# SyncE takes over 15 list fetches and 13 output writes of a graph network kernel, one row a transfer

## The chip, the cores and the metric

The kernel runs on one core of one Trainium2 chip. A core has a matrix engine (PE; its weight loads are listed as PEld), a vector engine (DVE), a scalar engine (ACT), GpSimd (POOL) and SyncE (SP), which computes nothing and issues DMA transfers. Each engine runs its own instructions in order and waits for the others by semaphores. A transfer that an engine issues is carried out by the core's 16 DMA engines.

The metric is the time of one execution on the device, in microseconds (us), as the median over several runs. Before the change it is 3867.69 us over nine runs, from 3839.4 to 3890.41.

## What is computed

A graph with N = 6250 nodes of 256 features and E = 100000 edges, sorted by their target node, goes through three attention layers. For each node they gather rows of the nodes that send it an edge, weigh them by a softmax, and add them up:

```python
# layers 1 and 2 (4 heads of 64, with a loop edge at each node)
xl, xr = x @ Wl, x @ Wr
logits = einsum('ehc,hc->eh', leaky_relu(xl[src] + xr[dst], 0.2), att)
alpha = softmax over the edges of one dst
out[dst] += alpha * xl[src]            # + b; elu after layer 1
# x = layernorm(x + layer 2)
# layer 3 (8 heads of 32)
e = leaky_relu(s1[src] + s2[dst], 0.2)
out[dst] += softmax(e) * Wh[src]
# result = layernorm(x + layer 3)
```

The result has one row of 256 f32 for each node, in the order of the nodes.

## The kernel before

**Plan.** `make_plan` sorts the nodes by their number of edges, most first, and cuts them into 49 blocks of 128, a node a partition. `cols[b]` is the number of edge columns of block b, fixed when the program is built: 27, 25, 24, 23, 22, 21, 21, 20, ... down to 9, 803 in all. What few edges the first block has beyond 27 go another way (`find_few`). `node_i[p, b]` holds the number of the node at partition p of block b. The DRAM table `near_d` has for each node, in the nodes' own order, its list of sources (CM = 38 numbers) followed by its row of x (256 f32): 1176 bytes. A tile `wrong` collects tests of the plan. If any fails, `fits` is 0 and a general path runs in place of `tile_by_degree`.

**Layer 1** (`layer2(0, ...)`). For block b, `start1(b)` has POOL fetch the block's 128 rows of `near_d` by an indirect DMA with `node_i` into `near[:, b, :]` (L1674), three blocks ahead of the work. `gather(b)` issues one indirect DMA on POOL for each column (L1300): 128 rows of a table into one slot of a row tile. Row tiles hold up to 9 columns; the pool has nine of them, so a block takes three (up to block 17) or two. `ready` has PE transpose the block's x rows and make its own terms, `attend` has DVE form the logits (z: L1571, L1591, L1594; lg: L1595) and ACT the exponentials (L1446), `weighted_sum` scales the rows (ACT L1482, DVE L1483) and adds them on PE (L1490), and `finish1` makes the two table rows of layer 2, which SP writes (L1708 and L1709). `finish` of block b - 1 and the last part of `weighted_sum` of block b stand in one round of the loop, the two writes at its end.

**Layer 2** (`layer2(1, ...)`) does the same with lists that are in SBUF by then. It is not touched by the change.

**Layer 3** is the last loop of `tile_by_degree`. A round b issues `gather(b + 1)` on POOL, then `put_out(b - 2)`, also on POOL: an indirect DMA that writes 128 rows of y to the result by `node_i` (L1812). DVE then forms logits (L1782), the products (L1503) and their sums (L1512), and in `between` the layer norm of the block before is made, with ACT writing y (L1534).

Nothing plans the order: `manual_schedule` keeps the instructions on each engine as the code issues them. Waits are put in by the framework. The transfers of SP and ACT go round eight semaphores, and each waits for the last one on its own.

Of the kernel before, what the change touches and what calls it, by code (L numbers as in the profile page):

```python
# [26 lines left out]
F32 = mybir.dt.float32  # L27
BF16 = mybir.dt.bfloat16
I32 = mybir.dt.int32
AF = mybir.ActivationFunctionType  # L30
OP = mybir.AluOpType
AX = mybir.AxisListType
# [3 lines left out]
P = 128  # L36
# [4 lines left out]
RUNS = 64  # L41
EARLY = (14, 12, 11)
LATE = 4


def columns(E, N, NB):

    mean = E / N
    pmf = [math.exp(-mean)]
    for k in range(1, 200):
        pmf.append(pmf[-1] * mean / k)
    over, sd = [], []
    for c in range(199):
        p = sum(pmf[c + 1 :])
        g = sum((k - mean) * pmf[k] for k in range(c + 1, 200))
        over.append(N * p)  # L60
        sd.append(math.sqrt(max(N * (p * (1.0 - p) - g * g / mean), 0.0)))
    cols = []
    for b in range(NB):
        most = P * b
        cols.append(next(
            c for c in range(199) if (over[c] + 3.5 * sd[c] <= most if b else over[c] < 0.01)
        ))
    low = max((c for c in range(199) if N - over[c] <= P // 4), default=0)
    high = next(c for c in range(199) if over[c] <= P // 4)
    pmf += [0.0] * 200  # L70
    held = next(
        c for c in range(199)
        if N * sum((k - c) * pmf[k] for k in range(c, 200))
        + 3.5 * math.sqrt(N * sum((k - c) ** 2 * pmf[k] for k in range(c, 200))) <= P
    )
    assert cols[1] <= held < cols[0]
    return cols, low, high, held


@with_exitstack  # L80
# [634 lines left out]
def make_plan(  # L715
# [6 lines left out]
    nc = tc.nc  # L722
    N, F = x.shape
    E = src.shape[0]
    NB = node_i.shape[1]
    NP = NB * P
    H2, D2 = att[0].shape[1], att[0].shape[2] - 1
    H1, _, D1 = w3.shape
    W2 = H2 * (D2 + 1)
    CM = max(cols)  # L730
    T = 16
    KE = -(-E // (P * T)) * T
# [19 lines left out]
    one = ctx.enter_context(tc.tile_pool(name="plan_one", bufs=1))  # L752
    tmp = ctx.enter_context(tc.tile_pool(name="weights", bufs=2))
    work = ctx.enter_context(tc.tile_pool(name="table1", bufs=3))
    rowp = ctx.enter_context(tc.tile_pool(name="table1_row", bufs=10))
    hot = ctx.enter_context(tc.tile_pool(name="plan_hot", bufs=2))
    ps = ctx.enter_context(tc.tile_pool(name="plan_ps", bufs=1, space=PSUM))
    pst = ctx.enter_context(tc.tile_pool(name="table1_ps", bufs=2, space=PSUM))
# [62 lines left out]
    xs, turned, at = {}, {}, [0]  # L821
# [52 lines left out]
    full, rest = divmod(E, KE)  # L874
# [23 lines left out]
    a = next(d for d in range(512, 0, -16) if E % d == 0)  # L898
# [222 lines left out]
    for k in range(BITS - 2, -1, -1):  # L1121
        n = CM + (1 << k) - 1
# [25 lines left out]
    for k in spans:  # L1148
# [8 lines left out]

    wrong = one.tile([P, KE + 2 * NB + 1], F32, name="wrong")  # L1160
    nc.vector.tensor_tensor(wrong[:, : KE - 1], dst_e[:, : KE - 1], dst_e[:, 1:], op=OP.is_gt)
    nc.vector.tensor_tensor(wrong[:, KE - 1 : KE], dst_e[:, KE - 1 :], next_e, op=OP.is_gt)
    nc.vector.tensor_tensor(wrong[:, KE : KE + NB], got[:, 2, :], most, op=OP.is_gt)
# [5 lines left out]
        wrong[:, KE + NB : KE + 2 * NB], wrong[:, KE + NB : KE + 2 * NB], count  # L1169
    )  # L1170
    nc.vector.tensor_scalar(
        wrong[:, KE + 2 * NB :], base[:, :1], float(E), None, op0=OP.not_equal
    )
    bad = one.tile([P, 2], F32, name="bad")
    nc.vector.reduce_sum(bad[:, :1], wrong, axis=AX.X)
# [32 lines left out]
def tile_by_degree(  # L1208
# [62 lines left out]
    nc.sync.dma_start(wh_d[NP:], nobody[:, 1, :A1])  # L1271


    bias = [fixed[:, 0, :], fixed[:, 1, :]]
    a_src, a_dst = fixed[:, 2, :], fixed[:, 3, :]

# [14 lines left out]

    def source(of, b, j):
        return bass.IndirectOffsetOnAxis(ap=of[:, b, j : j + 1], axis=0)

    def gather_rows(b, rows, cut, own, table, of, width, j0, j1):

# [239 lines left out]
    def layer2(i, table, of, width, start, own, finish, follow):  # L1536
# [5 lines left out]
        with ExitStack() as es:  # L1542
# [9 lines left out]
            def gather(b):  # L1552
# [4 lines left out]
                    gather_few(table, i, width)  # L1557
                state[b] = [rows, cut]

            later = []  # L1560

            def ready(b):
# [72 lines left out]
            for b in range(NB):  # L1635
                if b + 3 < NB:
                    start(b + 3)
                if b + 1 < NB:
                    gather(b + 1)
                if b + 2 == NB:  # L1640
                    follow()
                if b + 1 < NB:
                    ready(b + 1)
                rows, cut, wt, new = attend(b)
                if b:
                    rest = finish(work, pst, b - 1, acc)
                else:
                    new()
                    few = few_sum(work, pst, wt[0], cols[0] + 1, H2, D2 + 1)
                if b:  # L1650
                    new()

                last = []

                def between():
                    if b:
                        last.append(rest())

                acc = weighted_sum(
                    work, ps, rows, cut, wt, H2, D2 + 1, between,  # L1660
                    [bias[0]] if i == 0 else [x1[:, b, :], bias[1]], b == 0,
                )
                if b == 0:
                    nc.tensor.matmul(acc, edges_of, few, start=False, stop=True)
                if last:
                    last[0]()
            finish(work, pst, NB - 1, acc)()()

    def none(t):
# [1 line left out]
        nc.vector.memset(t.rearrange("p (h d) -> p h d", h=H2)[:, :, D2:], -BIG)  # L1671

    def start1(b):
        nc.gpsimd.indirect_dma_start(  # L1674
            out=near[:, b, :], out_offset=None, in_=near_d[:, :], in_offset=node(b)
        )
# [81 lines left out]
    with ExitStack() as es:  # L1758
# [32 lines left out]
        def end(b, acc, den):  # L1791
            h = work.tile([P, F], F32, name="h", bufs=2)
            nc.vector.tensor_mul(
                per_head(h, H1), per_head(acc, H1), den.unsqueeze(2).to_broadcast([P, H1, D1])
            )
            nc.vector.tensor_add(h, h, x1[:, b, :])
            mv, sd = spread_of(work, h)

            def rest():
                y = work.tile([P, F], F32, name="y")  # L1800
                layer_norm(y, h, mv, sd)
                return b, y

            return rest

        gap = work.tile([P, 1], F32, name="gap", bufs=1)
        prod = work.tile([P, 24, F], F32, name="weighted", bufs=1)

        def put_out(b, y, apart):
            if apart:  # L1810
                nc.gpsimd.memset(gap, 0.0)
            put = nc.gpsimd.indirect_dma_start(  # L1812
                out=out[:, :], out_offset=node(b), in_=y, in_offset=None,
                bounds_check=N - 1, oob_is_err=False,
            )
            tc.declare_no_dep(put.ins, group="out", reason="each node has a row of its own")
            tc.add_to_no_dep_group("out", put.ins)

        gather(0)
        acc, den, puts, rest = None, None, {}, None  # L1820
        for b in range(NB):
            if b + 1 < NB:
                gather(b + 1)
            if b - 2 in puts:
                put_out(*puts.pop(b - 2), apart=b + 1 == NB)
            rows, cut, wt, new = attend(b)
            if b:
                rest = end(b - 1, acc, den)
            den = new()
            nc.vector.reciprocal(den, den)  # L1830

            def between():
                if b:
                    puts[b - 1] = rest()

            acc = added_up(work, prod, rows, cut, wt, H1, D1, between)
            if b == 0:
                more = ps.tile([P, F], F32, name="few_acc", tag="tp")
                few = few_sum(work, ps, wt[0], cols[0], H1, D1)
                nc.tensor.matmul(more, edges_of, few, start=True, stop=True)  # L1840
                nc.vector.tensor_add(acc, acc, more)
# [31 lines left out]
```

## Time and profile before

| | us |
|---|---|
| median of 9 runs | 3867.69 |
| lowest, highest | 3839.4, 3890.41 |
| profiled execution | 3886.18 |
| its span | 3884.4 |

Over the span DVE was busy for 2754.9 us (71%), POOL for 2505.1 (64%), PE for 1549.4 (40%) and ACT for 1154.8 (30%). SP has no busy time, since issuing a transfer is not counted. The DMA engines moved 395.84 MB, 102 GB/s on average. The plan takes the first 134 us, layer 1 runs to about 1440, layer 2's first full gather stands at 1531 and its last at 2637, and layer 3's gathers run from 2727 to 3838.

How to read the profile: "busy" lines give an engine's share in 40 equal slices of the span, in tenths. A group's line has the code line, engine, operation, what it writes and reads, its count, then the busy time and the mean nanoseconds of one, then the engine's idle time before it and what ended most of that. A line of waits has who waited for whom, the total in us, the number of times and the longest. "issue" is time in which an engine waited for nothing that the profile shows. A line of a timeline has start, duration and the idle time before. A line of one code line's instructions has their count and shortest, median and longest duration in ns. A "q" after an engine's name marks its sequencer, which loads registers, waits and issues transfers.

### The profile page before, as it was taken

To read this page: it belongs to the slowest core of one execution; us is meant where nothing else is said; L and a number is where in the kernel's file an instruction comes from. 1 tells how busy PE (TensorE), PEld (TensorE's weight loads), DVE (VectorE), ACT (ScalarE), POOL (GpSimd) and SP (SyncE) were. 2 spreads that over 40 slices of the span, in tenths; PEclk is the share of its full clock that TensorE was granted. 3 is DMA by queue.
4 is the path that set the end of the run, shared out by engine and by line. 5 is a ranking of instruction groups with operands and counts; after the bars stand their busy time and mean duration, and the time that the engine had idled before them with its cause. 6 is when DMAs were issued, how large, how long until landed. Compare 5 with 4: busy or idle time off the path is not lost.

```text
span 3884.4 us, 24262 instructions
## 1 busy us (share of the span) xinstructions
PE 1549.4 (40%) x5424; PEld 1182.6 (30%) x5424; DVE 2754.9 (71%) x2527; ACT 1154.8 (30%) x4428; POOL 2505.1 (64%) x2588
## 2 busy tenths in 40 slices
PE   7234545536666774566564666665000000000000
PEld 5123444424555553444443444443000000000000
DVE  7546777747888885898886888885686566666665
ACT  3112333424445442343343555653000000000000
POOL 5565556656666645666666666654677777777774
PEclk8566777768888886677777777887555555555555
DMA  9633333333434433334443444433343333333332
GB/s 205 116 89 85 91 87 95 95 87 104 106 103 110 108 84 99 98 105 112 107 110 107 108 116 113 115 104 79 100 108 101 97 97 96 96 97 96 97 96 57
DMA packets 189103, 395.84 MB, mean 102 GB/s; under 512 B 56249, under 2 KB 107963, under 8 KB 188934
## 3 DMA queue, kind: packets, MB, share of 16 engines
q0 software_dynamic: 121392, 339.19, 33.6%
q1 hardware_dynamic: 59858, 53.27, 5.0%
q10 hardware_dynamic: 7700, 1.74, 0.4%
q8 instruction: 47, 0.77, 0.1%
q14 instruction: 106, 0.87, 0.1%
HBM read 354.02 MB, written 40.42 MB: 102 GB/s over the span
## 4 chain that ended last, share of the span: by engine, by line
issue 30%; POOL 23%; DVE 20%; PE 13%; ACT 6%; another core or an unknown queue 4%; DMA 3%; DVEq 0%; POOLq 0%; ACTq 0%; SPq 0%
POOL g L1300 21%; PE acc L1490 11%; DVE z L1594 4%; ACT g L1482 4%; DVE z L1571 4%; DVE lg L1595 3%; DVE z L1591 3%; DVE g L1483 2%; DMA g<-xl_d,near_r 2%; PE pm L1427 2%; POOL out L1812 1%; DVE weighted L1503 1%; POOL piece_of L1016 1%; ACT wt L1446 1%
## 5 line engine op out<-in xcount | busy, mean ns | idle before, releaser
L1300 POOL DMA_INDIRECT g<-xl_d,near_r x1569 | 1484.2, 946 | 881.5 <-issue 459.5
L1490 PE MATMUL acc<-g,ident 128*128 128x256 f32 x3408 | 1040.5, 472 | 800.6 <-issue 324.9
L1490 PEld LDWEIGHTS acc<-g,ident 128*128 128x128 f32 x3408 | 799.7, 241 | 1040.3 <-issue 351.8
L1300 POOL DMA_INDIRECT g<-whs_d,near_r x766 | 795.7, 1039 | 280.9 <-issue 247.7
L1482 ACT ACTIVATE g<-g,by 128x64 f32<-128x64 f32 x2308 | 609.5, 338 | 345.7 <-issue 337.8
L1595 DVE TENSOR_REDUCE lg<-z 128x28 f32<-128x1820 f32 (+4 forms) x234 | 497.3, 2125 | 8.1
L1594 DVE TENSOR_TENSOR z<-z,at 128x1820 f32<-128x1820 f32 (+4 forms) x234 | 496.8, 2123 | 4.7
L1512 DVE TENSOR_REDUCE acc_v<-weighted 128x256 f32<-128x4096 f32 (+15 forms) x49 | 343.7, 7014 | 14.7 <-remote 8.4
L1483 DVE TENSOR_TENSOR g<-g,wt 128x1792 f32<-128x1792 f32 (+8 forms) x234 | 331.7, 1434 | 27.9 <-issue 18.2
L1571 DVE TENSOR_TENSOR z<-g,pr 128x2080 f32<-128x2080 f32 (+4 forms) x96 | 197.9, 2061 | 177.8 <-DMA g<-xl_d,near_r 68.6
L1591 DVE TENSOR_TENSOR z<-g,pr 128x1820 f32<-128x1820 f32 (+3 forms) x138 | 299.6, 2171 | 17.0 <-DMA g<-xl_d,near_r 8.4
L1456 ACT ACTIVATE wt<-lg 128x128 f32<-128x128 f32 (+17 forms) x49 | 14.0, 285 | 854.2 <-DVE top L1439 314.2
L1671 DVE MEMSET pr<- 128x4 f32 x49 | 3.0, 62 | 348.5 <-remote 118.5
L1782 DVE TENSOR_TENSOR lg<-g,s_r 128x56 f32<-128x56 f32 (+4 forms) x111 | 22.2, 214 | 317.2 <-DMA g<-whs_d,near_r 275.3
L1503 DVE TENSOR_TENSOR weighted<-g,wt 128x1792 f32<-128x1792 f32 (+4 forms) x111 | 226.6, 2057 | 0.1
L1422 ACT COPY xT<-pt 128x256 f32<-128x256 f32 x147 | 54.9, 373 | 508.6 <-PE pt L1420 267.1
L1446 ACT ACTIVATE wt<-lg,top 128x19 f32<-128x19 f32 (+14 forms) x392 | 116.0, 296 | 93.9 <-DVE few_at L1607 34.3
L1427 PE MATMUL pm<-wcat,xT 128*128 128x260 f32 x392 | 109.9, 428 | 51.8 <-ACT xT L1422 41.7
L1427 PE MATMUL pm<-wh_cat,xT 128*128 128x272 f32 x196 | 75.8, 521 | 86.7 <-ACT xT L1422 58.7
L1427 PEld LDWEIGHTS pm<-wcat,xT 128*128 128x128 f32 x392 | 77.7, 209 | 75.6 <-ACT xT L1422 50.4
L1427 PE MATMUL pl<-wcat,xT 128*128 128x260 f32 x196 | 62.8, 448 | 78.1 <-issue 45.7
L1812 POOL DMA_INDIRECT out<-y,node_i x49 | 50.5, 1031 | 49.6 <-ACT y L1534 35.6
(250 smaller groups left out, 1665.8 us busy)
## 6 DMA issues: line engine op xcount, KB each, us to landing
g<-xl_d,near_r POOLq DMA_INDIRECT x1569
g<-whs_d,near_r POOLq DMA_INDIRECT x766
whs_d<-row SPq DMA_DIRECT2D x49, 132.0 KB
xl_d<-xl SPq DMA_DIRECT2D x49, 130.0 KB
xl_d<-row SPq DMA_DIRECT2D x49, 130.0 KB
xr_d<-row SPq DMA_DIRECT2D x49, 130.0 KB
two<-xl_d SPq DMA_DIRECT2D x49, 130.0 KB
two<-xr_d SPq DMA_DIRECT2D x49, 130.0 KB
```

The costliest lines, as they stand in the source:

```text
L1300: nc.gpsimd.indirect_dma_start(out=g[:, j + own - s0, :width], out_offset=None, in_=table, in_offset=source(of, b, j),)
L1427: nc.tensor.matmul(pm, xT[:, c, :], w[:, c, :], start=c == 0, stop=c == 1)
L1446: nc.scalar.activation(wt[:, :, h], lg[:, :S, h], AF.Exp, bias=top[:, h : h + 1], accum_out=den[:, h : h + 1],)
L1482: nc.scalar.mul(g4[:, t, h, :], g4[:, t, h, :], by[:, t - m, h : h + 1])
L1483: nc.vector.tensor_mul(g4[:, :m], g4[:, :m], wt[:, s0 : s0 + m, :].unsqueeze(3).to_broadcast([P, m, H, F // H]),)
L1490: nc.tensor.matmul(acc, ident, g4[:, t], start=False, stop=s0 + t == S - 1 and not more)
L1503: nc.vector.tensor_mul(prod[:, s0 - base : s1 - base, :].rearrange("p t (h d) -> p t h d", h=H), g[:, :n, :F].rearrange("p t (h d) -> p t ...
L1512: nc.vector.reduce_sum(part, prod[:, : s1 - base, :].rearrange("p s f -> p f s"), axis=AX.X)
L1571: nc.vector.tensor_max(z, rows[0][:, :n, :W2], xr[:, None, :].to_broadcast([P, n, W2]))
L1591: nc.vector.tensor_max(z, g[:, :n, :W2], xr[:, None, :].to_broadcast([P, n, W2]))
L1594: nc.vector.tensor_mul(z, z, at[:, None, :].to_broadcast([P, n, W2]))
L1595: nc.vector.reduce_sum(lg[:, s0:s1, :], z.rearrange("p t (h d) -> p t h d", h=H2), axis=AX.X)
```

## The change

Two functions choose blocks when the program is built. `rows_in` takes blocks of layer 1 from block 6 on as fast as 2.6 rows for each column of earlier blocks allow: 6, 8, 11, 13, 16, 18, 21, 24, 27, 30, 33, 36, 40, 43, 47. `rows_out` takes blocks of layer 3 with at least 128 / 2.6 = 49 columns between them: 0, 3, 6, 9, 12, 15, 18, 21, 25, 29, 33, 37, 41.

For these blocks POOL's indirect DMA goes, and SP moves each of the 128 rows by a transfer of its own: 1920 in layer 1 and 1664 in layer 3. The row's place in DRAM comes from a register. `row_starts` makes a tile of the places once in each of the two layers: `node_i` times the row's bytes on DVE, a transpose on PE, a copy on DVE, so that a block's 128 numbers stand in one partition. `numbers_of` has SP load 32 of them into registers at a time. The DRAM tensors are seen as bytes, so the number is the offset.

In layer 1 the rows are issued in the order of the blocks, `int(cols[b] * 2.6)` at the end of each round of the loop, behind that round's two table writes in SP's queue. In layer 3 a taken block's 128 rows are issued where its y is made, each with a `nop` before it. The y of taken blocks has a tile of its own, and the other blocks' y tiles go from three to two. One more test in `wrong` makes sure that no block but the last holds a number without a node.

```diff
+U8 = mybir.dt.uint8
+ALONG = 2.6
+def rows_in(cols):
+    taken, room = [], 0.0
+    for b in range(5, len(cols)):
+        room += cols[b - 5] * ALONG
+        if room >= P:
+            taken.append(b)
+            room -= P
+    return taken
+def rows_out(cols):
+    taken, free, past = [], 0.0, 0
+    for b, n in enumerate(cols):
+        past += n
+        if past >= free and sum(cols) - past >= P / ALONG + 2 * n:
+            taken.append(b)
+            free = past + P / ALONG
+    return taken
...
-    wrong = one.tile([P, KE + 2 * NB + 1], F32, name="wrong")
+    wrong = one.tile([P, KE + 3 * NB], F32, name="wrong")
...
+    nc.vector.tensor_scalar(
+        wrong[:, KE + 2 * NB + 1 :], node_i[:, : NB - 1], float(N), None, op0=OP.is_ge
     )
...
+    def row_starts(work, ps, turned, width, bufs):
+        scaled = work.tile([P, F], F32, name="h", bufs=bufs)[:, :NB]
+        nc.vector.tensor_scalar(scaled, node_i, float(width), None, op0=OP.mult)
+        flip = ps.tile([NB, P], F32, name="flip", tag="tp")
+        nc.tensor.transpose(flip, scaled, ident)
+        nc.vector.tensor_copy(turned, flip)
+    def numbers_of(turned, b, most):
+        for k in range(0, P, 32):
+            _, to = nc.values_load_multi_w_load_instructions(
+                turned[b : b + 1, k : k + 32], engines=[mybir.EngineType.SP],
+                min_val=0, max_val=most,
...
+            )
+            for j, v in enumerate(to):
+                yield k + j, v
+    def as_bytes(t):
+        return t.bitcast(U8).rearrange("n f -> (n f)").unsqueeze(0)
+    def rows_along(turned, blocks):
+        wide = 4 * (CM + F)
+        for b in blocks:
+            for p, v in numbers_of(turned, b, (N - 1) * wide):
+                nc.sync.dma_start(
+                    near[p : p + 1, b, :].bitcast(U8), as_bytes(near_d)[:, bass.ds(v, wide)]
+                )
+                yield
...
+            if i == 0:
+                turned = zp.tile([NB, P], I32, name="near_at")
+                row_starts(work, pst, turned, 4 * (CM + F), 3)
+                along = rows_along(turned, IN)
...
                 if last:
                     last[0]()
+                for _ in zip(range(int(cols[b] * ALONG)), along):
+                    pass
...
     def start1(b):
+        if b in IN:
+            return
         nc.gpsimd.indirect_dma_start(
...
-                y = work.tile([P, F], F32, name="y")
+                if b in OUT:
+                    y = work.tile([P, F], F32, name="y_rows", bufs=1)
+                else:
+                    y = work.tile([P, F], F32, name="y", bufs=2)
...
+        turned = numbers[:NB, :].bitcast(I32)
+        row_starts(work, ps, turned, 4 * F, 2)
+        def put_rows(b, y):
+            for p, v in numbers_of(turned, b, (N - 1) * 4 * F):
+                nc.sync.nop()
+                alone(nc.sync.dma_start(
+                    as_bytes(out)[:, bass.ds(v, 4 * F)], y[p : p + 1, :].bitcast(U8)
+                ))
...
-                    puts[b - 1] = rest()
+                    done_b, y = rest()
+                    if done_b in OUT:
+                        put_rows(done_b, y)
+                    else:
+                        puts[done_b] = (done_b, y)
```

## The prediction

> **What bounds the kernel now.** I read the page first, then the busy time by stage, the chain that ended last by stage, the waits by stage, and last what SyncE (SP) does. Times are us from the start of the span; rows are those of the kernel before. The page's busy slices show three stages: layer 1 (slices 2 to 16), layer 2 (to 28), layer 3 (the rest, where PE is idle).
>
> ```profile
> PE   7234545536666774566564666665000000000000
> DVE  7546777747888885898886888885686566666665
> POOL 5565556656666645666666666654677777777774
> ...
> L1300 POOL DMA_INDIRECT g<-whs_d,near_r x766 | 795.7, 1039 | 280.9 <-issue 247.7
> L1812 POOL DMA_INDIRECT out<-y,node_i x49 | 50.5, 1031 | 49.6 <-ACT y L1534 35.6
> ```
>
> Layer 3 is POOL's: its issues follow each other with 0.30 us between them, a put of a block's rows (L1812) among them. The chain that ended last says the same, in its line for 2727 to 3838, and the vector engine's waits there are for gathered rows:
>
> ```profile
> by line: POOL g L1300 53.6%; issue 35.7%; POOL out L1812 3.2%; DVE weighted L1503 2.7%; DMA g<-whs_d,near_r 1.0%; another core or an unknown queue 0.6%; DVE stats L1522 0.4%; DVE h L1796 0.4%; DVE h L1793 0.4%; DVE top L1439 0.4%; DVE lg L1
> ...
> DVE lg L1782 <- DMA g<-whs_d,near_r: 275.3, 35, 10.9
> ```
>
> Here a POOL instruction less is time saved. Layer 1 is different. The waits of 340 to 850, and then of 950 to 1300:
>
> ```profile
> PEld acc L1490 <- DVE row L1671: 136.3, 11, 16.0
> POOL g L1300 <- PE acc L1490: 128.5, 14, 20.8
> ...
> POOL g L1300 <- PE acc L1490: 37.7, 12, 3.3
> ```
>
> POOL waits for PE to release row tiles, once a block: I count 240 us of its idle time between layer 1's gathers beyond the 0.30, 3 us in almost every block from 3 on. PE in turn waits for DVE. Between 340 and 1440 the gathers landed hold back DVE little; the loop from the weights over ACT and PE back to DVE sets the pace. There a POOL instruction less is a longer wait for a tile.
>
> **The profiled execution** took 3886.18 (span 3884.4 and 1.8 around it), 18.5 above the median 3867.69 of nine runs. I work out differences against it and take them off the median.
>
> **What leaves POOL in layer 3.** Thirteen puts. The timeline of POOL gives one its price:
>
> ```profile
> 3188.03 1.09 POOL L1300 DMA_INDIRECT g<-whs_d,near_r  x1 [0.30 <-issue]
> 3189.43 1.02 POOL L1812 DMA_INDIRECT out<-y,node_i  x1 [0.30 <-issue]
> 3190.76 0.97 POOL L1300 DMA_INDIRECT g<-whs_d,near_r  x1 [0.30 <-issue]
> ```
>
> From 3189.43 to 3190.76 is 1.33; 13 x 1.33 = 17.3. DVE idles 8 to 11 us in most blocks here (L1782), so it can follow. The last taken block is 41 and the stretch after the last gather (3837.7 to 3884.4) has none of them: it stays.
>
> **What leaves POOL in layer 1.** Fifteen fetches (blocks 6 to 47), 15 x (0.946 + 0.30) = 18.7 of POOL's time. I cost the gain at 0: POOL has 2.5 to 20 us of waiting for tiles in those blocks. If I read the loop wrongly it is up to 18.7.
>
> **What SP gets: 1920 row transfers in layer 1, 1664 in layer 3.** The program has no transfer placed by a register, so a row's price r is bounded by its parts:
>
> ```profile
> L886 SPq DMA_DIRECT2D dst_e<-in_dst x1: 223/223/223, 2.4 to 2.4; - x1
> ...
> L1271 SPq EVENT_SEMAPHORE  x1: 17/17/17, 131.1 to 131.1; - x1
> L1271 SPq DMA_DIRECT2D whs_d<-nobody x1: 237/237/237, 131.2 to 131.2; - x1
> ...
> L700 SPq TENSOR_LOAD <-fits x1: 472/472/472, 128.6 to 128.6; - x1
> L700 SPq FUSED_REGOPS  x1: 181/181/181, 129.1 to 129.1; - x1
> ```
>
> A transfer with one run a side holds SP 0.223 to 0.237, its semaphore 0.017. Low end: one load serves 32 registers at the price of one, 0.472/32 = 0.015, and no arithmetic: r = 0.27. High end: each register pays a whole load (0.663, L707's on SP) and arithmetic (0.181): r = 1.10. I take 0.2 a register, under the quickest whole load (0.290, L707 on ACT), because 32 share one instruction, and no arithmetic, because the numbers in the tile are byte offsets already: r = 0.46. The nop of layer 3 adds a 0.02 to 0.03 like an event semaphore.
>
> A second limit: the trace's records show SP's and ACT's transfers going round eight semaphores (41 or 42 transfers each), each waiting for the one eight before it. From issue to last update the median is 2.1 (L1708, a write) and 2.8 (L1717, a read) for 130 KB; an eighth is 0.26 to 0.35 a row, under r, though it takes over if a row's landing exceeds 3.7.
>
> The Trainium skill's Runtime: NRT & Kernel Launch (Instruction fetch mechanics) puts register loads at about 200 ns a register even in bulk. It describes loads from HBM, and the trace's single loads do not show a bulk one; by it r would be 0.24 + 0.02 + 0.20 = 0.46, an estimate. DMA: Bandwidth & Descriptors (Rules for kernel authors) speaks against the change: gather many small transfers into one, since under 64 KB one pays mostly overhead. This trace shows the same gap: POOL pays 1.25 for 128 rows in one issue, SP would pay 128 x 0.46 = 59. By the rule, end to end at the 2.1 to 2.8 of the two rows above, 3584 transfers would take 7500 us and more and the kernel would be several times slower; by eight in flight it is a row each 0.26 to 0.35.
>
> **Has SP the time?** In layer 1 SP writes two tables a block and waits for ACT in between:
>
> ```profile
> 1103.14 0.32 SPq L1709 DMA_DIRECT2D xr_d<-row  x1
> 1123.03 0.32 SPq L1708 DMA_DIRECT2D xl_d<-row  x1
> 1123.90 0.32 SPq L1709 DMA_DIRECT2D xr_d<-row  x1
> 1143.75 0.32 SPq L1708 DMA_DIRECT2D xl_d<-row  x1
> ```
>
> Rows stand in SP's queue after these writes, int(2.6 x columns) a block: 39 where a block has 15 columns. 39 x 0.46 = 18 fits the 19.5 to 19.9 shown; the two writes behind them go out late by nothing. I walked SP through all 49 blocks at the old times, each write no earlier than it was, a block's rows landed 2.5 after its last. Between a block's second write and the next block's first, SP is free for 0.55 to 0.66 a row up to block 12 and for 0.50 to 0.56 after block 26; what one block lacks, lag carries to the next. A late row holds POOL at that block's first gather, and every gather behind it; before DVE suffers, 37 to 71 us pass (from the first tile's last gather to DVE's first use, 42 at block 43). The walk gives: r up to 0.55, no loss; 0.60, 50; 0.65, 122; 0.70, 218; 0.80, 410; 1.10, 990. The table writes held in SP's queue would hold ACT too (three row tiles), which is in the same lag. The rows end in block 43, so SP is empty before layer 2's first gathers need the tables.
>
> In layer 3 SP has nothing else. A taken block's y has one tile, so its 128 rows must be gone before the next taken one: 980 us from block 1's last gather to block 42's, less 17, over 12 x 128 rows is 0.63 a row, 0.57 at the tightest (18 to 21). A single shortfall holds ACT and then DVE, while POOL runs on in its nine tiles (four blocks, some 80 us). Block 41's rows start near 3724 and take 61: 80 before the end. Regular y tiles fall from three to two: y of block b needs the put two blocks earlier, which is issued at 3163.08 where y is written at 3170.77; 5 us of cover after some 2.5 of landing, without that cover a block starts up to 2.5 later.
>
> **Small terms.** The scaling, transpose and copy of the numbers: DVE 2 x 0.18 (as L1404), PE 0.27, twice. In layer 1 DVE then waits 24.1 for block 0's lists (L1308), in layer 3 POOL 27.7 for the last table row; uncovered, 1 each. The added column test: 0.2 at most, before layer 1. Consumers of a block's lists now wait for eight semaphores, not one: at 0.017 to 0.028 each, on PE and ACT, at most 15 x 0.4 = 6; mostly behind waits they have anyway, I take 2. Rows share the DMA engines, busy 0.37 to 0.41 in layers 1 and 2; 3584 more small transfers are a few per cent unless they all fall on one engine, which POOL-bound layer 3 would see only at its end.
>
> Sum: -17.3 + 0 + 2 = -15.3 on 3886.2 gives 3871 profiled; 3867.7 - 15.3 = **3852**.
>
> **Rivals.**
> 1. SP cannot keep up in layer 1 (slower than before). It decides from r = 0.56, where the walk's loss eats the 15. For it: 0.31 a register, a whole quick load (0.290 to 0.318), is enough, or one 0.154 to 0.181 of arithmetic a row. Against: 32 loads in one instruction. At r = 0.65: 3852 + 122 = 3974; at 0.60, 3902.
> 2. Layer 1 gains as well: 3852 - 18.7 = 3833. For it: POOL is on the chain of 340 to 1440 with 4.3%. Against: its wait for PE in each block.
> 3. The puts leave POOL but nothing comes of it: waits for the y tile, or gathers slowed by SP's rows, give the 17 back: about 3868. Against: DVE's idle 8 to 11 a block.
>
> **How the numbers follow.** Forecast 0.58, SP too slow 0.30, layer 1 too 0.07, nothing gained 0.05. The forecast's own range is 3840 to 3862 (small terms 0 to 8 off 17 and a few of layer 1). 0.5% is 19.3, about what a measurement of this kernel can tell from no change; -15 lies inside it, so the forecast splits: about two fifths beyond -19, the rest within. Faster 0.07 + 0.23 = 0.30; within 0.35 + 0.03 = 0.38; slower, nearly all of rival 1 and a little of 3, 0.32. The range 3830 to 3970 holds the forecast, rival 2, 3, and rival 1 up to r = 0.65, half of it.
>
> **What would show it.** In the profile after: POOL's out at L1812's successor x36 and its list fetch x34; from layer 3's first to last gather 17 less; layer 1 as long as before, POOL's wait for PE a microsecond longer in the taken blocks. SP's rows 0.4 to 0.5 apart. Wrong if rows stand 0.6 or more apart and POOL's gathers wait for a landing on near, or if DVE's first use of a block waits for rows in layer 1.

## The result: 1.18 times as long, and the profile after

The changed kernel took 4579.92 (median of ten runs, 4564.86 to 4587.82) beside 3869.61 for the kernel before: a ratio of 1.1836, 95% interval 1.1808 to 1.1865. The forecast was 3852, its range ended at 3970.

The page of the kernel after, first the busy slices of two engines, then its costliest groups as in the profile before:

```profile
DVE  7555565556564655878877888838244444544445
POOL 4654444454454443666666666557455444455543
...
L1364 POOL DMA_INDIRECT g<-xl_d,near_r x1569 | 1483.3, 945 | 1235.3 <-PE acc L1554 543.0
...
L1901 POOL DMA_INDIRECT out<-y,node_i x36 | 36.7, 1021 | 511.9 <-ACT y L1598 505.5
...
L1598 ACT ACTIVATE y_rows<-h,sd 128x256 f32<-128x256 f32 x13 | 7.8, 600 | 901.4 <-DMA out<-y_rows 899.2
```

The puts are down to 36 as they should be, but in layer 1 (slices 2 to 16) and in layer 3 (from slice 27) POOL and DVE both work less densely than before. The stages, by the first and last gather of each:

| us | before | after | difference |
|---|---|---|---|
| up to layer 1's first gather | 134.8 | 132.6 | -2.2 |
| layer 1, first to last gather | 1302.9 | 1640.3 | +337.4 |
| on to layer 2's first full gather | 93.8 | 88.7 | -5.1 |
| layer 2 | 1105.9 | 1107.2 | +1.3 |
| on to layer 3's first | 90.0 | 91.7 | +1.7 |
| layer 3 | 1110.4 | 1483.3 | +372.9 |
| last gather to the end | 46.6 | 43.5 | -3.2 |

The waits of the kernel after in layer 3 (3060 to 4544), who for whom, total, times, longest:

```profile
ACT y_rows L1598 <- DMA out<-y_rows: 899.2, 12, 115.5
DVE den L1523 <- ACT wt L1520: 713.7, 13, 94.2
POOL out L1901 <- ACT y L1598: 481.8, 12, 54.0
```

ACT cannot write the next taken block's y until the 128 rows before it are out; DVE waits for ACT, and POOL's put for ACT. So layer 3 goes at the pace of SP's rows. The chain that ended last can be followed back only to 4372 here, so it covers the last 172 of this stretch, and the shares below, taken of the whole stretch, add up to little. In what there is of it SP's rows come first, where POOL's gathers did before:

```profile
by line: SPq L1894 4.7%; issue 4.2%; POOL g L1364 1.3%; SPq L1339 0.6%; DVE weighted L1567 0.2%; DMA out<-y_rows 0.2%; POOL out L1901 0.1%; ACT y_rows L1598 0.1%; DVE h L1866 0.0%; DVE top L1503 0.0%; DVE lg L1855 0.0%; DVE lg L1859 0.0%; A
```

In layer 1 few waits are put down to the rows themselves: POOL waits 101.7 for their landing, in four waits. The two largest waits of POOL and ACT between 340 and 1770 are others:

```profile
POOL g L1364 <- PE acc L1554: 421.8, 35, 24.5
ACT xT L1486 <- remote: 301.7, 36, 42.3
```

"Remote" is something the profile cannot name; before, it held ACT's copies of xT for 31.0. How much of the 337 comes from late rows and how much from table writes that stand behind rows in SP's queue was not separated.

What a row costs SP shows in all instructions of the line of the puts (shortest, median and longest in ns, first and last start):

```profile
L1894 SPq MOVE out<-y_rows x1664: 1/29/1401, 3063.6 to 4581.0; - x185
L1894 SPq DMA_DIRECT2D out<-y_rows x1664: 1/228/1397, 3115.1 to 4581.1; - x185
```

A row is two instructions, a register move of 0.029 and the transfer's issue of 0.228, and 0.32 from row to row at best. But some take 0.70 or 1.40 each, the move too, and in such stretches rows stand 2.1 to 2.8 apart. A block's 128 rows took 80 to 181 in layer 3, mostly about 105, and 87 to 124 in layer 1 from the third taken block on. From one row's move to the next, register loads included and waits over 5 left out, the mean is 0.69 in layer 1 and 0.88 in layer 3. In layer 3 most slow stretches begin 5 to 11 after a run of POOL's gathers begins and end some 7 after it ends; where POOL has idled longer, rows go at 0.32.

All of this holds for one of two conditions in which chips were met. On four of the seven chips that the comparisons fell on, the kernel before took 3860 to 3910; on the other three it took 3330, with the program unchanged. The last section of the experiments uses the second; everything else is of the first.

### The profile page after: what moved, and what is told of

It is laid out like the page before. It is cut to its first block, busy times and chain, and to the rows that moved or that the text cites. A ratio compares the mean times of both kernels' runs of the same rounds, so it can differ in the third digit from the quotient of the medians.

```text
span 4587.3 us, 31735 instructions
## 1 busy us (share of the span) xinstructions
PE 1605.1 (35%) x5426; PEld 1218.3 (27%) x5426; DVE 2753.7 (60%) x2532; ACT 1137.7 (25%) x4428; POOL 2408.9 (53%) x2560
## 3 DMA queue, kind: packets, MB, share of 16 engines
q14 instruction: 164, 1.34, 0.1%
## 5 line engine op out<-in xcount | busy, mean ns | idle before, releaser
L1364 POOL DMA_INDIRECT g<-xl_d,near_r x1569 | 1483.3, 945 | 1235.3 <-PE acc L1554 543.0
L1364 POOL DMA_INDIRECT g<-whs_d,near_r x766 | 728.2, 951 | 260.4 <-issue 226.4
L1546 ACT ACTIVATE g<-g,by 128x64 f32<-128x64 f32 x2308 | 592.8, 337 | 225.1 <-issue 218.2
L1523 DVE TENSOR_REDUCE den<-wt 128x8 f32<-128x128 f32 (+17 forms) x49 | 13.3, 272 | 713.7 <-ACT wt L1520 713.7
L1901 POOL DMA_INDIRECT out<-y,node_i x36 | 36.7, 1021 | 511.9 <-ACT y L1598 505.5
L1486 ACT COPY xT<-pt 128x256 f32<-128x256 f32 x147 | 54.8, 373 | 804.4 <-remote 453.3
L1491 PE MATMUL pm<-wcat,xT 128*128 128x260 f32 x392 | 129.3, 486 | 186.7 <-issue 119.1
L1491 PE MATMUL pl<-wcat,xT 128*128 128x260 f32 x196 | 81.2, 554 | 190.5 <-issue 99.4
L1491 PEld LDWEIGHTS pm<-wcat,xT 128*128 128x128 f32 x392 | 88.6, 237 | 214.4 <-issue 125.4
```

Of the source, the lines that this page charges most:

```text
L1364: nc.gpsimd.indirect_dma_start(out=g[:, j + own - s0, :width], out_offset=None, in_=table, in_offset=source(of, b, j),)
L1491: nc.tensor.matmul(pm, xT[:, c, :], w[:, c, :], start=c == 0, stop=c == 1)
L1546: nc.scalar.mul(g4[:, t, h, :], g4[:, t, h, :], by[:, t - m, h : h + 1])
```

## The experiments

**Theory A**: SP's rows are slow only while POOL issues gathers closely, whatever SP itself does; each part of the change then loses by itself, because SP's average is above what the forecast's walk allowed. **Rival B**: the two parts hurt together. **Rival C**: a row simply costs some 0.85, gathers or not.

### Each part alone

```diff
-    IN, OUT = rows_in(cols), rows_out(cols)
+    IN, OUT = rows_in(cols), []
```

> Only the 1920 row fetches of layer 1, all 49 puts of layer 3 back on POOL. Theory A (the two parts cost by themselves, each because SP's rows slow down while POOL issues gathers): layer 1 about 335 longer as in the changed kernel, the rest as before, total about 3870 + 335 - 5 = 4200, between 4170 and 4230. Rival B (the two parts hurt together, for instance by the length of SP's program): clearly under 4150.

```diff
-    IN, OUT = rows_in(cols), rows_out(cols)
+    IN, OUT = [], rows_out(cols)
```

> Only the 1664 row writes of layer 3, all list fetches of layer 1 back on POOL. Theory A: layer 3 about 373 longer as in the changed kernel (the 17 of POOL's puts already in it), total about 4240, between 4210 and 4270. Rival B: clearly under 4190, and the sum of this excess and that of the layer 1 part falls short of 710.

Layer 1's part alone took 4208.4 (ratio 1.0888, 1.0836 to 1.0939), layer 3's alone 4232.5 (1.0946, 1.0899 to 1.0993). The excesses add up to 0.183, that of both together. Rival B is out.

### Rows without anyone waiting for them

```diff
+    IN, OUT = [], rows_out(cols)
...
-                    y = work.tile([P, F], F32, name="y_rows", bufs=1)
+                    y = x1[:, b, :]
```

> As the layer 3 part alone, but a taken block's y goes into its own place (the block's slice of x1, which nobody reads any more), so no block waits for the rows before it. Theory A (a row costs SP some 2.1 to 2.8 while POOL gathers and 0.33 to 0.39 while it doesn't): POOL's gathers are never held and run in about 1110 - 17 = 1093 as the forecast had it; SP gets through some 400 to 500 of the 1664 rows by then, and 1150 to 1250 rows are left for after the last gather, at 0.39, some 450 to 490; total about 4270 (4220 to 4330). Rival C (a row costs about 0.85 on average whatever POOL does): the gathers also run in 1093, but some 1250 rows are gone by the last gather and the rest takes 0.85 each after it; total about 4230, and rows after the last gather stand 0.85 apart. If the gathers themselves are slowed by rows (rival D), they take clearly more than 1120.

It took 4329.5 (1.1182, 1.1127 to 1.1236). The gathers of layer 3 ran in 1092.4, where the forecast's sum has 1110.4 - 17.3 = 1093.1: so taking the puts from POOL does gain what was said. So rows do not slow the gathers (rival D). But SP was through only three blocks by the last gather (3777), and the other ten, 1280 rows where up to 1250 had been expected, went out behind it. The same line of code while POOL gathers (3110 to 3450) and after the last gather (3870 to 4270):

```profile
L1894 SPq DMA_DIRECT2D out<-near_r x120: 5/700/1401, 3110.6 to 3447.3; - x120
L1894 SPq MOVE out<-near_r x120: 4/700/1400, 3112.0 to 3448.7; - x120
...
L1894 SPq DMA_DIRECT2D out<-near_r x1001: 227/228/274, 3870.0 to 4269.8; - x167
L1894 SPq MOVE out<-near_r x1000: 29/29/29, 3870.2 to 4269.7; - x167
```

340 for 120 rows is 2.8 each; 400 for 1000 is 0.40, the register loads included. One line of code, two prices seven times apart. Rival C falls. What differs is that POOL gathers in the first stretch and not in the second; but the other engines work in the first stretch too, which the kernel of its own below takes away.

### Three puts, far apart

```diff
-    IN, OUT = rows_in(cols), rows_out(cols)
+    IN, OUT = [], [3, 17, 31]
```

> Only three puts in layer 3 go to SP, blocks 3, 17 and 31, some 290 to 350 apart in time. Theory A: a block's rows take up to 128 x 2.5 = 320 while POOL gathers without a break, which just fits, so nothing waits for long; total 3870 - 4 = 3866 (3855 to 3890), rows 2.1 to 2.8 apart nearly throughout. Rival C (0.85 a row whatever POOL does): the same total, but each block's rows done in about 110.

3866.7, ratio 0.9975 (0.9951 to 0.9999), the rows of the first two blocks 2.8 apart (358 and 356 for 128). With room for that price nothing is lost.

### What slows beside gathers: a kernel of its own

```python
KINDS = [("a", "none", "row"), ("b", "wide", "row"), ("c", "thin", "row"), ("d", "fill", "row"),
    ("e", "act", "row"), ("f", "wide", "nops"), ("h", "wide", "same"), ("i", "wide", "small"),
    ("j", "none", "small"), ("k", "apart", "row"), ("l", "none", "nops")]
```

> A kernel of its own that computes none of the three layers (its output is a copy of x): eleven sections with a barrier between them, in each of which SP issues 64 row fetches of 1 KB placed by registers, beside something else. (a) nothing beside; (b) POOL gathers of 128 rows of 1 KB back to back; (c) the same gathers with rows of 64 bytes; (d) POOL fills of SBUF, no DMA; (e) ACT issues plain transfers of 128 rows of 1 KB, POOL idle; (f) as b, with eight nops ahead of each of SP's rows; (h) as b, SP's rows from fixed addresses, so no register move; (i) as b, with 120 small activations, memsets and matmuls on ACT, DVE and PE in place of SP's rows; (j) those alone; (k) gathers with POOL fills between them, half as dense; (l) as f with no gathers. All theories: a and d 0.32 to 0.39 a row. Theory A1 (SP's issues compete with POOL's for making descriptors): b and c 2.1 to 2.8 a row, e 0.3 to 0.4, h as b, i as j on all engines. Theory A2 (every instruction of an engine's queue takes 0.7 to 1.4 beside gathers): b 2.8, f 2.8 + 8 x 0.7 = 8 or more, h 1.4, i's small activations 1.4 apart against 0.1 to 0.3 in j. Theory A3 (it is each recorded start and end that takes 0.70, so that instructions the trace doesn't record cost nothing): b 2.8, f as b, h 1.4, i as in A2. If bytes count, c is fast; if the number of packets counts, c is as b and e is slow too; if POOL's issuing counts, c is as b and e is fast.

| section | a row of SP, us |
|---|---|
| a, nothing beside | 0.32 |
| b, gathers of 1 KB rows | 0.32 for the first 17, then 2.8 |
| c, gathers of 64-byte rows | 2.8 |
| d, POOL fills | 0.32, once section c's slow stretch had passed |
| e, ACT's plain transfers | 0.49 median, mean 0.70, no step of 0.70 |
| f, eight nops a row | up to 14.0, then 0.80 once the gathers were over |
| h, fixed addresses; k, gathers 1.69 apart | rows over in 29 and 23, before a slow stretch could set in or last |

The nops of (l) were not in the compiled program, so it adds nothing to (a). In f, 14.0 is ten instructions (eight nops, move, transfer) at 1.40. So it is every instruction, not the transfer; and neither bytes (7 GB/s in c) nor DMA traffic as such (222 GB/s in e) makes it. Section i has no SP rows. The groups there (1279 to 1425), and those of j without gathers (1544 to 1559):

```profile
L116 ACT ACTIVATE small<-little 128x16 f32<-128x16 f32 x116 | 24.9, 215 | 599.7 <-remote 479.5 <-ACT small L116 114.2 <-issue 5.5
...
L117 DVE MEMSET gate<- 128x1 f32 x119 | 7.0, 59 | 139.4 <-issue 120.7 <-DVE gate L117 16.2 <-remote 1.5
```

```profile
L116 ACT ACTIVATE small<-little 128x16 f32<-128x16 f32 x61 | 13.1, 215 | 116.4 <-SPq L88 114.5
L117 DVE MEMSET gate<- 128x1 f32 x118 | 7.0, 59 | 52.2 <-SPq L88 44.4
```

Some 118 instructions took DVE 146 in the first and 15 in the second; each still lasts 59 ns, it is the time between them that grows. ACT ran 13 and DVE 16 of them at full pace and then one per 1.40, PE 42 pairs of load and matmul and then a pair per 2.8. It is not SP's matter at all: here every engine but POOL is held to an instruction per 1.40, after a few that go at full pace.

### How close the gathers must be

```python
KINDS = [("p0", P, 0), ("p1", P, 1), ("p2", P, 16), ("p3", P, 128), ("p4", P, 256),
    ("p5", P, 512), ("p6", P, 1024), ("q64", 64, 0), ("q96", 96, 0)]
```

> A kernel of its own as the one before (no layer is computed): nine sections, in each 192 row fetches of 1 KB by SP beside 100 gathers by POOL. p0: gathers of 128 rows back to back (1.25 to 1.40 apart). p1 to p6: a fill of 1, 16, 128, 256, 512, 1024 numbers a partition on POOL after each gather, which puts the gathers 1.3 to 2.5 apart. q96 and q64: back to back, but of 96 and of 64 rows. Theory A2a (the slow mode is there when the gathers' transfers never drain, some 1.40 for 128 rows, so that something every engine needs for each instruction comes through once per gather): p0 slow (2.8 a row); from a distance of about 1.45 to 1.6 on all rows 0.33 to 0.39; q64 fast (half the rows fit into 0.7), q96 (1.05) fast. Theory A2b (it is POOL's issuing itself, whatever it moves): q64 and q96 as slow as p0, and p1 to p6 rows get slower or faster smoothly with the share of POOL's time in gathers: at 2.5 apart still some 1.4 a row.

| | gathers apart, us: mean (median) | rows apart 25 us into the section |
|---|---|---|
| p0, back to back | 1.25 (1.25) | 2.76 |
| p1, p2, p3 | 1.38, 1.38, 1.39 (1.25, 1.26, 1.34) | 1.54, 1.53, 1.51 |
| p4, p5, p6 | 1.44, 1.66, 2.08 (the same) | 0.39, 0.38, 0.38 |
| q64, q96 | 1.20, 1.22 (the same) | 2.82, 2.84 |

POOL's busy time, the granted clock, the DMA engines' share and GB/s in stretches of p3, p4 and q64:

```profile
706.00:818.00 112.00, 93.02 (x161) 1.00 0.33 94
880.00:930.00 50.00, 44.21 (x69) 1.00 0.34 95
1414.00:1508.00 94.00, 70.18 (x79) 1.00 0.22 55
```

There is a step between p3 and p4, that is between 1.34 and 1.44 by the median, with POOL as busy and the DMA engines as loaded on either side (p3 and p4), and gathers of half the rows slow SP as much with 55 GB/s. So both forms of the theory were half right: a step, as A2a said, but set by how closely POOL issues, as A2b said, and not by what is moved. POOL itself seems not to be free of it: in p1 to p3 most gathers stand at their section's shortest distance, but 22 to 34 of 99 follow 1.38 to 2.8 after the one before, which lifts the mean; in the other sections all distances but the odd one are alike.

### Spacing the gathers in the kernel

```diff
+                if pace[0] and b > 2:
+                    nc.gpsimd.memset(few_row[:, :256], 0.0)
```

After each gather POOL fills a tile that nobody reads; gathers then stand 1.45 apart in the trace. First in layers 1 and 3 of the changed kernel (the expectation's 839 counts 37 gathers that stand ahead of layer 3's first):

> The changed kernel with a fill of 256 numbers a partition on POOL after each gather of layers 1 and 3 (from block 3 on), which puts the gathers some 1.44 apart or more; SP's rows as in the changed kernel. Theory A (SP is slow only beside gathers less than about 1.4 apart): rows 0.33 to 0.39 throughout, no block waits for rows; layer 1 takes 1300 to 1340 as in the kernel before, layer 3 is POOL's at 839 x 1.44 = 1210 where it was 1110; total 3970 to 4010, some 580 faster than the changed kernel although POOL does more. Rival C (the rows' price does not hang on the gathers' distance): the fills only add to it, 4600 to 4750.

4000.7, ratio 1.0242 (1.0208 to 1.0275) to the kernel before, which took 3905.7 on that chip. The changed kernel has 1.18: with more work on POOL it is 0.16 of the time before faster. Layer 3 takes 1156 instead of 1483, a row 0.48 on average, and ACT's wait for the rows out of y_rows (899 before) is gone. The total is in the expected range, but by luck: layer 1 takes 1426 where 1300 to 1340 was expected, at 0.70 a row, and layer 3's 1156 makes up for part of it. So theory A holds for layer 3 here and not for layer 1.

> Only the 1920 row fetches of layer 1, with the fill after each gather of layer 1; layers 2 and 3 as in the kernel before. Theory A: 3860 to 3910, against 4208 without the fills. Rival C: 4210 to 4350.

3982.9 (1.0183, 1.0134 to 1.0232): a miss, though 225 less than without the fills. Layer 1 takes 1421.9, a row 0.70 on average, about as without fills (0.72 with the lists alone, 0.69 in the changed kernel). So theory A's "slow only below 1.4" is too simple for layer 1: with a fill and a gather in each 1.45, SP's rows were still held there, in steps of up to 1.4. The fills nevertheless took 202 off layer 1 (1624.1 with the lists alone). In the kernel before, without rows, they took 49 off it, as the next run shows, by freeing the other engines; what makes up the rest was not separated.

> The kernel before with the fill after each gather of layer 1. POOL gets 750 x 0.19 = 143 more work there and has 240 of waits for PE. If ACT's activations, 1.40 apart in the kernel before beside gathers, cost layer 1 something, it gets 10 to 60 shorter: 3810 to 3860. If they cost nothing, or POOL's waits are needed where they are, it gets 0 to 60 longer: 3870 to 3930.

> As the one before, with the fill in layer 2 too. There POOL's 800 gathers stand 1.38 apart on average, so at 1.44 it takes 1156 for the gathers alone where layer 2 took 1106: 30 to 70 longer than the kernel with the fill in layer 1 alone, unless the other engines gain more than that.

The kernel before with fills in layer 1 took 3833.7, a ratio of 0.9818 (0.9788 to 0.9847), 72 less than the kernel before on that chip where 10 to 60 less was expected; with layer 2 as well 0.9869 (0.9839 to 0.9898). The fill in layer 2 cost 17.5, less than the 30 to 70 expected. Layer 1 went from 1302.9 to 1253.9. The same group of ACT's (340 to 1385), before and with fills:

```profile
L1482 ACT ACTIVATE g<-g,by 128x64 f32<-128x64 f32 x852 | 227.7, 337 | 148.3 <-issue 146.8
```

```profile
L1486 ACT ACTIVATE g<-g,by 128x64 f32<-128x64 f32 x900 | 222.4, 335 | 9.3 <-issue 7.5
```

POOL's wait for PE in that stretch went from 184.3 to 34.7. So the slow pitch already held the kernel before: in layer 1 of its trace 122 of 988 of these activations, of 0.34, stand 1.40 behind the one before, after a wait that it calls "issue".

### Where the slow pitch is absent

Two kernels were next compared together: the one with fills again, and one with room for SP.

```diff
-ALONG = 2.6
+ALONG = 1.6
...
-    IN, OUT = rows_in(cols), rows_out(cols)
+    IN, OUT = rows_in(cols), [3, 17, 31]
```

> The changed kernel with fewer of SP's rows and with the fill after each gather of layer 1: 1.6 rows a column in place of 2.6, so nine blocks of layer 1 (8, 11, 15, 20, 24, 29, 34, 40, 46), and three puts of layer 3 (3, 17, 31). SP has some 0.9 to 1.1 a row in layer 1, and rows took 0.64 there beside spaced gathers (82 a block), so none is late. Layer 1 with the fills alone took 1254, and 803 gathers and 49 fetches at 1.45 make 1235 of it, so POOL sets it and nine fetches less are worth up to 9 x 1.45 = 13; three puts 4. Theory A: 5 to 20 faster than the kernel before with fills in layer 1, run beside it, some 0.978 of the kernel before. Rival E (SP's rows cost the block loop something even when they are in time, for instance by waits on eight semaphores): as the kernel with fills or up to 20 slower.

> The kernel before with the fill after each gather of layer 1, once more, on the same chip as the kernel with fewer rows: 0.979 to 0.985 of the kernel before, as it was.

The comparison fell on a chip of the second condition: the kernel before took 3330.4, the fills alone 3454.3 (1.0367, 1.0353 to 1.0381), fewer rows with fills 3434.6 (1.0313, 1.0298 to 1.0327). So both expectations against the kernel before missed: there the fills only cost. Moving nine fetches and three puts away gains 19.7 of that, the top of what theory A had. The changed kernel itself came next:

> The changed kernel, unchanged, beside the kernel before, on whichever chip it falls. In the comparison before this one the kernel before took 3330 on its chip, not 3870, and SP's rows stood 0.32 apart beside gathers 1.25 apart in layer 3. If it falls on such a chip: Theory A says that rows at 0.39 with their register loads fit into what SP has (0.5 a row in layer 1, 0.6 in layer 3), so the forecast's sum holds: POOL's 17 in layer 3 gained, up to 19 in layer 1, 0.989 to 0.999 of the kernel before. Rival C (rows cost too much for a reason other than the slow pitch beside gathers): clearly above 1.02. If it falls on a chip where the kernel before takes 3860 to 3910: 1.17 to 1.19 again, and nothing new.

This one fell on a chip of the first condition: 4590.6, ratio 1.186 (1.18 to 1.1919). Then:

> The kernel with nine blocks and three puts for SP and the fill after each gather of layer 1, once more. Where the kernel before takes 3860 to 3910: 0.974 to 0.984 of it, by theory A (0.9818 was measured there for the fills alone, and nine fetches and three puts are worth up to 17). Where it takes 3330: 1.025 to 1.037 again, since the fills only cost there.

> The changed kernel, unchanged. Where the kernel before takes 3330 and SP's rows are not slowed beside gathers: theory A 0.989 to 0.999 of it, rival C clearly above 1.02. Where the kernel before takes 3860 to 3910: 1.17 to 1.19 as before.

Second condition: fewer rows with fills 1.0315 (1.0298 to 1.0332), and **the changed kernel 3309.3 against 3330.4, a ratio of 0.9942 (0.9925 to 0.9958)**. The line of the puts there, to be held against that of the profile after:

```profile
L1894 SPq MOVE out<-y_rows x1664: 29/29/29, 2269.9 to 3244.8; - x185
L1894 SPq DMA_DIRECT2D out<-y_rows x1664: 227/228/313, 2324.8 to 3244.8; - x185
```

Not one slow instruction in 1664 rows, with gathers back to back beside them; 128 rows take some 49 with three of their four register loads (2.17 each at the median) in it, 0.40 a row with all four.

> The kernel before, unchanged, for its stages where the slow pitch is absent. If it falls on such a chip (3330): ACT's activations of the weighted sum show no idle time to speak of (1 or 2 in layer 1, as in the kernel with fills there), against 171 in the profile before; layer 1's gathers take some 1070 to 1090 against the changed kernel's 1061 there, layer 3's 1022 against 1004. By the forecast's sum layer 1 gains nothing (rival 2: up to 19). If it falls on the other kind, it is the profile before once more.

It fell on a third such chip and took 3332.3, in one execution. ACT's activations in layer 1, first in the profile before (134 to 1438) and then here (131 to 1215), where they have no gaps:

```profile
L1482 ACT ACTIVATE g<-g,by 128x64 f32<-128x64 f32 x988 | 263.8, 337 | 171.3 <-issue 169.5
L1482 ACT ACTIVATE g<-g,by 128x64 f32<-128x64 f32 x1004 | 244.8, 334 | 1.5
```

The stages, from one profile each, on two chips of this condition (layer 1's gathers in the kernel before stay under the 1070 to 1090 expected):

| us, second condition | before | changed | difference |
|---|---|---|---|
| up to layer 1's first gather | 133.6 | 130.7 | -2.9 |
| layer 1, first to last gather | 1063.7 | 1061.0 | -2.7 |
| on to layer 2's first full gather | 69.1 | 54.8 | -14.3 |
| layer 2 | 962.8 | 962.0 | -0.8 |
| on to layer 3's first | 56.1 | 61.9 | +5.8 |
| layer 3 | 1022.1 | 1004.0 | -18.1 |
| last gather to the end | 23.0 | 31.3 | +8.3 |

POOL's waits in the kernel before there (500 to 1200) are:

```profile
POOL g L1300 <- issue: 146.0, 479, 0.3
POOL near_r L1674 <- issue: 10.4, 34, 0.3
POOL g L1300 <- PE acc L1490: 5.8, 19, 0.3
```

No wait is longer than the 0.3 between any two gathers: POOL sets layer 1's pace here. DVE's logits in the changed kernel come earlier block by block, by 3.0 at first and about 17.5 from 940 on. There POOL does wait once for rows, 13.6 for those of the last taken block, which is why its last gather comes only 2.7 earlier; DVE's lead outlasts that wait.

POOL's gathers of layer 3 in the kernel before, here:

```profile
L1300 POOL DMA_INDIRECT g<-whs_d,near_r x766 | 727.9, 950 | 233.4 <-issue 228.2
```

In the first condition they lasted 1039 on average (795.7 in all, the longest 2.188). So POOL too is slower there in that condition, by 68 of the 88 that layer 3 is shorter here; that the same thing holds it was not tested.

## Why the prediction was wrong, step by step

- **The failed step is the price of a row on SP**, the r of the prediction. It was bounded by single instructions at rest (0.27 to 1.10) and taken as 0.46. At rest it is lower: 0.32 and a thirty-second of a load, 0.39 to 0.40. But beside gathers, which is where all rows are, it is up to 2.8, above the high end; and the average, with POOL stopping for SP now and then, came to 0.69 in layer 1 and 0.88 in layer 3. A price put together from the rows of idle stretches says nothing of a stretch in which another engine slows every instruction.
- **Rival 1 is half of what happened.** It has SP too slow in layer 1, and its threshold of 0.56 stands on the right side of all runs: at 0.40 to 0.48 nothing was lost to rows in the total, at 0.69 and more much. The walk has 218 lost at 0.70; measured were 337 at 0.69 and, with fills, 168 at 0.70 (1421.9 against 1253.9 with the fills alone). It is right in size only, since it held the old times for everything else, and the slow pitch and the fills change those too. Layer 3's loss of 373, the larger half, stands in no rival and not in the range, which ended at r = 0.65 (for which the walk has 3974, just outside).
- **Layer 3's tolerance** of 0.63 a row was right as a condition: at 0.88 the layer went at SP's pace, at 0.48 (fills) and 0.40 (second condition) it did not.
- **The 17 of the puts** were there: 18.0 in the gathers where no block waited for rows, 18.1 in the second condition. Of these 8.3 came back after the last gather, which the forecast left as it was.
- **Layer 1 at 0** was argued from POOL's waits for PE, which are in the profile; no run shows it, since rows were late in layer 1 in every run of the first condition that had them there. In the second condition POOL doesn't wait for PE, and layer 1 up to layer 2's first gather got 17.0 shorter, the 18.7 of rival 2. So 21 faster there agrees with the sum of 15 only by total: 17 came from where none was counted, and layer 3 with its end gave 9.8.
- **A register load** at 0.2 was too dear: 2.15 for 32 is 0.067. The Trainium skill's figure of about 200 ns a register (Runtime: NRT & Kernel Launch, Instruction fetch mechanics) does not hold for this load; the page speaks of loads from HBM, and this one is from SBUF. Its rule to gather small transfers into one (DMA: Bandwidth & Descriptors, Rules for kernel authors) pointed the right way in the first condition, though not for the reason it gives: with eight in flight, SP waited 13 from 340 on in all of layer 1 for landings of rows.
- **The sign that was passed over** stood in the profile before: 171 of ACT's idle time in layer 1 put down to "issue" with activations 1.40 apart, "issue" at the head of the chain of 340 to 1440 with 35.0%, and layer 3's gathers at a mean of 1039 ns where those of layers 1 and 2 took 946. The gaps of an engine that waits for nothing and yet stands still got no row in the prediction; SP's rows met the same 0.70 and 1.40.

**What stays open.** What holds the instructions, why only on some chips, and why gathers 1.45 apart left SP free in the kernel of its own but not in layer 1. Two things are seen. In slow stretches an issue that never takes under 0.22 in the second condition is recorded with 0.001 to 0.15 (380 of 3584 rows, 159 of them straight after an instruction of 0.6 or more), and 17 of 112 register loads, 2.03 and more there, with 0.003 to 1.76, as if the stamps of start and end were written late; and moves last one or two steps of 0.70. That speaks for the writing of the records as what is held, but nops were recorded too, so no run separates it from the instructions themselves. Whether an execution that is not profiled has the slow pitch can't be told from these runs. The Trainium skill (NOTIFIC — the notification-queue block, Overflow: three behaviours, one of which stalls the engine) says that the queue of such records can be set to stall the engine that writes to it; no run here shows it. The fewer rows with fills were not measured in the first condition, so no version is known to beat the kernel before in both.

## What to carry to other kernels

Before work is moved to an engine's queue, look in the trace at the pitch of simple instructions on *any* engine beside what will run there; an engine that idles on "issue" for multiples of one step is a price list for the newcomer. Many small instructions on a second queue are cheap only while the first leaves room for them: bound their price by the stretch they will stand in, not by the shortest row. And when two versions are compared, run the kernel before on the same chip: a gain of 1.8% in one condition was a loss of 3.7% in the other.

## What the runs showed of the hardware that was not expected

- Where indirect DMAs of POOL stood 1.20 to 1.34 apart, on four of seven chips SP came down to an instruction per 0.70 or 1.40; on the one chip where all were tried, ACT, DVE and PE did too, after 13 to 16 at full pace on ACT and DVE. At 1.44 and more SP was free of it where nothing else ran, but not in layer 1. POOL's own gathers in layer 3 lasted 1039 ns instead of 950. It did not matter whether a gather moved 64 or 128 rows, or 64 bytes or 1 KB a row.
- On the other three chips nothing of it was seen, and the same kernel took 3330 in place of 3870: layer 1 1063.7 for 1302.9, layer 2's 962.8 for 1105.9, layer 3's 1022.1 for 1110.4.
- A load of 32 registers from SBUF takes SP some 2.15, a transfer of one row placed by a register 0.029 + 0.228, and one row to the next 0.32.
